# A graph layer's kernel: the edge lists are squeezed in pieces through a PSUM bank, partly in an earlier stage, and ScalarE scales most of the node rows

## The chip, the cores and the metric

One core of one Trainium2 chip runs the whole program. The metric is the device time of one execution, in microseconds; the smaller the better.

## The reference

The layer has 12,500 nodes of 256 features and 212,500 edges, sorted by destination. Every node has a self loop.

```python
deg_out = clip(segment_sum(ones, src), 1)
deg_in  = clip(segment_sum(ones, dst), 1)
h  = feats * rsqrt(deg_out)[:, None]
m  = segment_sum(h[src], dst) * rsqrt(deg_in)[:, None]
x  = (m @ W_gc + b_gc) + (feats @ W_res + b_res)
y  = x + moe_ff(x)              # 64 experts, top 2, capacity 1024, 256 -> 512 -> 256, gelu
y  = (y - mean(y, 0)) * rsqrt(var(y, 0) + eps) * gamma + beta
out = layernorm(feats + y)      # over the features
```

All data are float32 and the indices int32.

## The kernel before

The program goes through five stages, one after the other.

1. Degree stage. The out-degrees are counted with one-hot matrices: VectorE makes `o_hi` and `o_lo` (L204), ScalarE makes `s_lo` (L421), TensorE multiplies them into `deg` and `deg_s`. Meanwhile SP's queue fetches the node features into `acc` (seen as `xs`) and writes zeros to DRAM, for `z_d` and for a strip `lent_d` (L431). At its end a short chain goes from one engine to the next: `s_sb` (L451), a last matmul, `d_out` (L454), a square root on ScalarE and a few small VectorE steps up to `r_out` (L193 to L199). `r_out` holds one over the root of each node's out-degree.
2. h stage. `xs` is multiplied by `r_out` in fifteen pieces of up to seven tiles of 128 nodes. VectorE does ten pieces (L542) and ScalarE five (L540, one instruction for each tile). Each piece is written to `h_d` in DRAM by SP (L544). The edge lists are fetched into a tile `room` (`Lanes.fetch`, L477 to L482), and VectorE runs `fitting` over them, which finds out whether the edges keep to the shape that the fast path needs. Once its rows are written out, `acc` is cleared for the sums (L558), ten parts by GpSimd and four by VectorE. A branch (L562) that is not taken on these data holds the slow path.
3. Edge stage. This is the longest. For each of 1,584 rows of 128 edges, GpSimd issues an indirect DMA (L702) that gathers 128 rows of `h_d` into a ring of six tiles of four rows. VectorE makes a one-hot matrix `o` (L694), 16 rows ahead. TensorE multiplies them into `p` (L716). Twelve rows make a group of nodes; its sums go through `out_of`, `add_own` (L762), `numbers`, `turn` and `to_nodes` (L815) into `acc`. When nodes are complete they go through the dense layer and the router (`nodes`, with L916 reading a PSUM bank), which enters the tokens into a PSUM table `tab` (L1016).
4. The experts, over tokens gathered from DRAM.
5. The two normalisations, and the output.

The edge stage's order is written out by hand in a `manual_schedule`: the loop over rows `c` records `row(c)`, `one_hot(c + 16)` and whatever `at_row` or `later` has put down for that row. The earlier stages are ordered by the scheduler. Every engine runs its own list in order.

The edges fall in two kinds. The first 168 rows (`HC`) are taken as they come. The other 118 groups (`NL`) are "lanes" of 1,620 edges (`L`) on one partition each, from which 84 self loops (`SKIP`) are taken out so that 1,536 edges are left; the self loops are added by `add_own`. That is the squeeze: an edge's source, place and mark are packed into one int32 word, the number of places it has to move is put in the top bits, and for each of seven bits (`BITS`) four operations move the words that have the bit set by 1, 2, 4, ... places. In the kernel before all of it is done in `compact()` (L1024 to L1077), as 46 VectorE steps on whole lanes, with every operand in SBUF. `compact_by` spreads them over the rows 14 to 109 of the edge stage. The lists are fetched a second time for this, into the end of `acc` (`lent`), which is filled from `lent_d` with zeros again at row 138 (L1128). Then TensorE turns the result over (`lay`), and ScalarE writes it to `src_col` and `rel` (`laid`), which the gathers and one-hots of row 168 and later read.

```python
lambda i=i: V.tensor_scalar(m, w, 31 - SHIFT - i, 31,
    op0=ALU.logical_shift_left, op1=ALU.arith_shift_right),
lambda: V.tensor_tensor(b, w, m, op=ALU.bitwise_and),
lambda: V.tensor_tensor(w, w, b, op=ALU.bitwise_xor),
lambda by=by: V.tensor_tensor(w[:, : L - by], w[:, : L - by], b[:, by:], op=ALU.bitwise_or),
```

`tables` is an SBUF tile that the router fills late. Until then parts of it serve as the source of zeros, as room for `own_of` and as room for `shift` in `numbers`.

Of the kernel before, what the change touches and what calls it, by code (L numbers as in the profile page):

```python
# [8 lines left out]
F32 = mybir.dt.float32  # L9
# [10 lines left out]
P = 128  # L20
# [33 lines left out]
ROOM = 3 * L + 2 * HALF  # L54
NC = NG * GR
W = P
# [45 lines left out]
def gnn_moe_kernel(  # L102
# [26 lines left out]
    lent_d = dram.tile([P, ROOM], F32, name="lent_d")  # L129
# [118 lines left out]

    with ExitStack() as stack:
# [24 lines left out]
        for a in range(0, ROOM, 2 * D):  # L274
            n = min(2 * D, ROOM - a)
            zeros.append((lent_d[:, a : a + n], zero[:, :n]))


        def columns():
# [14 lines left out]
            for k, to in enumerate((src_col, rel)):  # L294
                S.copy(to[:, :HC], p[:, k].rearrange("p a c -> p (a c)")[:, :HC])

# [99 lines left out]
        for c0 in range(0, C0 + 1, CH):  # L396
# [16 lines left out]
            for k in range(k0, k1):  # L413
# [23 lines left out]
                if k == 30:  # L437
                    columns()
                if k == 40:
                    windows()  # L440
# [16 lines left out]

    lent = acc[:, 2 * NP - ROOM :]  # L460

    class Lanes:
        def __init__(self, room):
            self.given = [room[:, i * L : (i + 1) * L].bitcast(I32) for i in range(2)]
            self.buf = room[:, 2 * L : 3 * L]

            self.left = room[:, 3 * L : 3 * L + HALF].bitcast(BF16)[:, : L + 1]
            self.at = room[:, 3 * L + HALF :].bitcast(BF16)[:, :L]
            self.is_self, self.again = (
                self.buf.bitcast(BF16)[:, i * L : (i + 1) * L] for i in range(2)  # L470
            )

        def fetch(self):
            b = HE + (NL - 1) * L
            for i, e in enumerate((src, dst)):
                t = self.given[i]
                GP.memset(t, (0, BEHIND)[i])  # L477
                nc.sync.dma_start(t[: NL - 1], e[HE:b].rearrange("(p c) -> p c", c=L))
                nc.sync.dma_start(
                    t[NL - 1 : NL, : M - b], e[b:].rearrange("(p c) -> p c", p=1)  # L480
                )
            GP.memset(self.left, 0.0)  # L482

        def leave_out(self, n_left):

            r = NL
            s, d = (t[:r] for t in self.given)
            is_self, again = self.is_self[:r], self.again[:r]
            return [
                lambda: V.tensor_tensor(is_self, s, d, op=ALU.is_equal),  # L490
                lambda: V.tensor_tensor(again[:, 1:], d[:, 1:], d[:, :-1], op=ALU.is_equal),
                lambda: V.tensor_tensor(again[:, 1:], is_self[:, 1:], again[:, 1:], op=ALU.mult),
                lambda: V.scalar_tensor_tensor(
                    self.left[:r, 1:L], is_self[:, :-1], 0.5, again[:, 1:],
                    op0=ALU.is_lt, op1=ALU.mult, accum_out=n_left[:r],
                ),
                lambda: V.tensor_scalar(
                    self.at[:r], d, n0_lane[:r], 255.0,
                    op0=ALU.subtract, op1=ALU.min,
                ),  # L500
            ]

    def fitting(lanes, n_left):

        r = NL

        def outside(i, lim_of, op):
            V.tensor_scalar(
                lanes.is_self[:r], lanes.at[:r], lim_of, None, op0=op, op1=ALU.add,
                accum_out=bad[:r, 2 + i : 3 + i],  # L510
            )

        def begins():
            junk = lanes.buf[:r, :r]
            V.scalar_tensor_tensor(
                junk, n0_b[:r, 0, HG:], 1.0, ident[:r, :r],
                op0=ALU.mult, op1=ALU.mult, accum_out=n0_lane[:r],
            )

        return [begins] + lanes.leave_out(n_left) + [  # L520
            lambda: outside(0, 0.0, ALU.is_lt),
            lambda: outside(1, float(W), ALU.is_ge),
            lambda: V.tensor_single_scalar(
                bad[:r, 4:5], n_left[:r], SKIP - 0.5, op=ALU.is_lt
            ),
        ]

    with ExitStack() as stack:
        two = stack.enter_context(tc.tile_pool(name="h_two", bufs=2))
        ps2 = stack.enter_context(tc.tile_pool(name="h_ps2", bufs=2, space=PSUM))  # L530
        one = stack.enter_context(tc.tile_pool(name="h_one", bufs=1))
        lanes = Lanes(one.tile([P, ROOM], F32, name="room"))
        lanes.fetch()
        n_left = one.tile([P, 1], F32, name="n_left")
        for i, (t0, n) in enumerate(GROUPS + [(NT - 1, 1)]):
            r = rows(t0)
            xt = xs[:r, t0 : t0 + n]
            if i % 3 == 1:
                for t in range(n):
                    S.activation(xt[:, t], xt[:, t], AF.Copy, scale=r_out[:r, t0 + t : t0 + t + 1])  # L540
            else:
                V.tensor_mul(xt, xt, r_out[:r, t0 : t0 + n, None].to_broadcast([r, n, D]))  # L542
            if r == P:
                nc.sync.dma_start(whole(h_d)[:, t0 : t0 + n], xt)  # L544
            else:
                nc.sync.dma_start(h_d[t0 * P :], xt[:, 0])
        for f in fitting(lanes, n_left):
            f()
# [8 lines left out]
        for i, t in enumerate(range(0, 2 * NT, 14)):  # L557
            (GP if i < 10 else V).memset(acc[:, t * P : (t + 14) * P], 0.0)  # L558
# [3 lines left out]
        with tc.If(unfit > 0):  # L562

# [39 lines left out]
            nc.sync.dma_start(lent_d, lent)  # L603

    lanes = Lanes(lent)
    lanes.fetch()


    with ExitStack() as stack:
# [117 lines left out]
        n_left = one.tile([P, 1], F32, name="n_left")  # L727

# [39 lines left out]
        def numbers(g, s, t):  # L768
            add_own(g, s, t)
            shift = spare[:, (5 + g // 2 % 2) * D : (6 + g // 2 % 2) * D]  # L770
# [74 lines left out]
        def nodes(t0, n, t):  # L845
# [168 lines left out]
            def enter(i, k, at, vals, t):  # L1014
                for m in range(2):
                    T.matmul(  # L1016
                        tab, vals[:r, m], at[:r],
                        start=t0 + i + k + m == 0, stop=t0 + i == NT - 1 and k + m == 2,
                    )
# [4 lines left out]
        def compact():  # L1024

            r = NL
            w, m = (t[:r] for t in lanes.given)
            before_, b, f = m.bitcast(F32), lanes.buf[:r].bitcast(I32), lanes.buf[:r]
            lf, ones_l = lanes.left[:r], lanes.is_self[:r]
            out_steps = lanes.leave_out(n_left) + [  # L1030
                lambda: V.memset(ones_l, 1.0),
                lambda: V.tensor_tensor_scan(
                    before_, ones_l, lf[:, :L], 0.0, op0=ALU.mult, op1=ALU.add
                ),
                lambda: V.scalar_tensor_tensor(
                    lf[:, :L], before_, SKIP + 0.5, lf[:, :L], op0=ALU.is_lt, op1=ALU.mult
                ),

                lambda: V.scalar_tensor_tensor(
                    f, lf[:, 1:], float(MARK), lanes.at[:r], op0=ALU.mult, op1=ALU.add  # L1040
                ),
                lambda: V.scalar_tensor_tensor(
                    w, w, float(2 * MARK), f, op0=ALU.mult, op1=ALU.add
                ),

                lambda: V.tensor_scalar_min(b, before_, float(SKIP)),
                lambda: V.scalar_tensor_tensor(
                    w, b, SHIFT, w, op0=ALU.logical_shift_left, op1=ALU.bitwise_or
                ),
                lambda: V.tensor_scalar_add(b, lf[:, :L], -1.0),  # L1050
                lambda: V.tensor_tensor(w, w, b, op=ALU.bitwise_and),
            ]
            for i in range(BITS):
                by = 1 << i
                out_steps += [
                    lambda i=i: V.tensor_scalar(
                        m, w, 31 - SHIFT - i, 31,
                        op0=ALU.logical_shift_left, op1=ALU.arith_shift_right,
                    ),
                    lambda: V.tensor_tensor(b, w, m, op=ALU.bitwise_and),  # L1060
                    lambda: V.tensor_tensor(w, w, b, op=ALU.bitwise_xor),
                    lambda by=by: V.tensor_tensor(
                        w[:, : L - by], w[:, : L - by], b[:, by:], op=ALU.bitwise_or
                    ),
                ]
            full = slice(0, GR * P)
            out_steps += [
                lambda: V.tensor_scalar(
                    m[:, full], w[:, full], 9, (1 << 14) - 1,
                    op0=ALU.arith_shift_right, op1=ALU.bitwise_and,  # L1070
                ),
                lambda: V.tensor_single_scalar(
                    b[:, full], w[:, full], 2 * MARK - 1, op=ALU.bitwise_and
                ),
                lambda: V.tensor_copy(before_[:, full], m[:, full]),
                lambda: V.tensor_copy(f[:, full], b[:, full]),
# [458 lines left out]
```

## Time and profile before

| | us |
|---|---|
| median of 3 runs | 3423.75 (3421.28 to 3424.61) |
| the profiled execution | 3423.65 |
| its span, first to last instruction | 3421.9 |
| first gather of the edge stage issued (L702) | 246.66 |
| last gather issued | 2282.63 |
| VectorE busy over the span | 1641.3 (48%) |
| GpSimd busy over the span | 2051.2 (60%) |
| TensorE busy over the span | 2685.0 (78%) |

The profile gives, for each engine, the busy time in forty slices of the span; for each group of instructions (a source line, an engine, an operation and a shape) the count, the busy time and the mean; and what ended the idle time before them. The trace behind it can be listed instruction by instruction. PE is TensorE, DVE is VectorE, ACT is ScalarE, POOL is GpSimd, and SP is the queue that issues most transfers. PEclk is the granted TensorE clock as a share of full speed. An indirect DMA shows as a POOL instruction for the time that GpSimd takes to issue it, not for the transfer.

### The profile page before, as it was taken

Reading aid. Unit: us, or ns where it says so; the run is one execution under the profiler, and the core shown is the slowest. Engines: PE = TensorE matmul, PEld = TensorE weight load, DVE = VectorE, ACT = ScalarE, POOL = GpSimd, SP = SyncE. Lnnn points to the kernel's source line nnn. Section 1 sums busy time; section 2 is a strip of 40 time slices with the busy share of each in tenths; the row PEclk is TensorE's granted clock in tenths of the full one; section 3 lists DMA queues with packets and bytes.
Section 4 is the critical chain, followed back from the end, with each engine's and each line's share of the span. In section 5 each row is a group of like instructions: output and inputs, shape, how many; then the busy total and the mean of one; then the engine's idle time right before and its main releaser. Section 6 shows DMA issues by size and latency. Waiting matters only on the chain. (4 is left out here: it accounts for less than half of the span.)

```text
span 3421.9 us, 36966 instructions
## 1 busy us (share of the span) xinstructions
PE 2685.0 (78%) x11059; PEld 1778.3 (52%) x11121; DVE 1641.3 (48%) x6013; ACT 707.9 (21%) x1994; POOL 2051.2 (60%) x2092
## 2 busy tenths in 40 slices
PE   6826777777787777777777778876999999999644
PEld 5612344444454544444444445554778766778533
DVE  9975534455445445545454455664222212222498
ACT  8930010000010000000000000111222211222368
POOL 0038877777777777777777777754555555554100
PEclk8755578888888888888888988888999999999865
DMA  9462244444444444444444444433344444566677
GB/s 356 158 200 77 85 156 123 125 126 127 128 126 126 127 124 126 128 129 126 122 129 126 126 127 130 131 97 119 111 131 126 133 153 154 178 183 203 214 221 238
DMA packets 257102, 498.19 MB, mean 146 GB/s; under 512 B 44567, under 2 KB 169109, under 8 KB 248578
## 3 DMA queue, kind: packets, MB, share of 16 engines
q0 software_dynamic: 98800, 264.95, 26.8%
q1 hardware_dynamic: 144800, 218.02, 19.5%
q10 hardware_dynamic: 13298, 12.80, 1.2%
q8 instruction: 91, 1.49, 0.2%
q14 instruction: 113, 0.93, 0.1%
HBM read 402.59 MB, written 96.44 MB: 146 GB/s over the span
## 5 line engine op out<-in xcount | busy, mean ns | idle before, releaser
L702 POOL DMA_INDIRECT ring<-h_d,src_col x1584 | 1553.8, 981 | 483.3 <-issue 424.6
L716 PE MATMUL p<-ring,o 128*128 128x258 f32 x3168 | 1207.3, 492 | 473.2 <-DMA ring<-h_d,src_col 436.8
L716 PEld LDWEIGHTS p<-ring,o 128*128 128x128 f32 x3168 | 619.0, 227 | 976.8 <-DMA ring<-h_d,src_col 666.0
L694 DVE TENSOR_SCALAR o<-lane,rel 128x128 f32<-128x128 f32 x1584 | 380.8, 303 | 617.4 <-PE p L716 617.3
L1275 PE MATMUL yp<-w,h 128*128 128x256 f32 (+3 forms) x1928 | 432.9, 380 | 0.0
L1231 POOL DMA_INDIRECT xg<-x_d,tables x241 | 233.0, 967 | 333.1 <-PE xtp L1246 219.4
L1259 PE MATMUL hp<-xT,w 128*128 128x384 f32 (+11 forms) x1328 | 399.4, 454 | 1.4 <-DVE xT L1250 1.4
L1275 PEld LDWEIGHTS yp<-w,h 128*128 128x128 f32 (+3 forms) x1928 | 341.3, 181 | 65.0 <-issue 7.3
L751 ACT COPY s<-p 128x258 f32<-128x258 f32 x132 | 49.4, 374 | 1325.1 <-PE p L716 1325.1
L1263 ACT ACTIVATE h<-hp,w 128x384 f32<-128x384 f32 (+11 forms) x332 | 181.2, 546 | 669.6 <-PE hp L1259 668.8
L1259 PEld LDWEIGHTS hp<-xT,w 128*128 128x128 f32 x1328 | 248.0, 191 | 131.6 <-issue 57.0
L1281 POOL DMA_INDIRECT z_d<-yo,tables x241 | 238.1, 988 | 121.9 <-DVE yo L1280 66.1
L1250 DVE COPY xT<-xtp 128x768 f32<-128x768 f32 (+2 forms) x83 | 77.4, 932 | 405.2 <-PE xtp L1246 405.2
L1280 DVE TENSOR_TENSOR yo<-yp,bb 128x256 f32<-128x256 f32 (+3 forms) x241 | 102.0, 423 | 276.3 <-PE yp L1275 268.5
L421 ACT ACTIVATE s_lo<-lane_b,nb 128x128 bf16<-128x128 bf16 x581 | 171.1, 389 | 4.4 <-DVE lo_end L412 1.8
L1016 PE MATMUL tab<-at,vals 128*128 128x512 bf16 x330 | 130.2, 471 | 18.2 <-DVE vals L1009 7.7
L815 DVE TENSOR_TENSOR acc<-q,acc 128x256 f32 x132 | 55.8, 423 | 165.5 <-PE q L792 122.0
L902 PE MATMUL bank<-wcat,acc 128*128 128x320 f32 x392 | 132.6, 464 | 0.0
L907 PE MATMUL bank<-wcat,xT 128*128 128x320 f32 x392 | 124.4, 440 | 0.0
L477 POOL MEMSET room<- 128x1620 int32 x2 | 2.8, 1447 | 192.7 <-DVE r_out L199 192.7
L711 ACT CAST ring<-mark 128x4 f32<-128x4 bf16 x354 | 57.8, 197 | 260.1 <-issue 260.0
L423 PE MATMUL deg<-o_hi,o_lo 128*128 128x98 bf16 x1079 | 79.9, 237 | 24.6 <-DVE o_lo L204 22.1
(280 smaller groups left out, 2583.8 us busy)
## 6 DMA issues: line engine op xcount, KB each, us to landing
w<-in_wpack SPq DMA_DIRECT2D x64, 1026.0 KB
ring<-h_d,src_col POOLq DMA_INDIRECT x1584, 2.8
z_d<-tables SPq DMA_DIRECT2D x98, 256.0 KB
zt<-z_d SPq DMA_DIRECT2D x24, 1024.0 KB
tables<-h_d SPq DMA_DIRECT2D x118, 128.0 KB
xt<-in_x ACTq DMA_DIRECT2D x48, 256.0 KB
x_d<-y SPq DMA_DIRECT2D x48, 256.0 KB
z<-in_x SPq DMA_DIRECT2D x12, 1024.0 KB
```

Of the source, the lines that this page charges most:

```text
L421: S.activation(s_lo[:, i], lane_b, AF.Sign, bias=nb[:, k, i : i + 1])
L694: o_last[u] = V.tensor_scalar(o_of[u][:, j], lane, rel[:, c : c + 1], None, op0=ALU.is_equal)
L702: i = GP.indirect_dma_start(out=r[:, k, :D], out_offset=None, in_=h_d, in_offset=bass.IndirectOffsetOnAxis(ap=src_col[:, c : c + 1], axis=0),)
L716: i = T.matmul(p_of[g], o_of[v][:, n], r[:, k], start=j == 0, stop=j == GR - 1)
L902: T.matmul(gps[i][:r], acc2[:, k, a : a + r], wcat[:, k], start=k == 0, stop=False,)
L907: T.matmul(gps[i][:r], v["xT"][:, i, k, :r], wcat[:, 2 + k], start=False, stop=k == 1,)
L1016: T.matmul(tab, vals[:r, m], at[:r], start=t0 + i + k + m == 0, stop=t0 + i == NT - 1 and k + m == 2,)
L1231: GP.indirect_dma_start(out=g, out_offset=None, in_=x2_d, in_offset=bass.IndirectOffsetOnAxis(ap=at[:, 0, k : k + 1], axis=0),)
L1259: T.matmul(hp[:, :m], w1[:, c, j * P : (j + 1) * P], xT[:, c, :m], start=c == 0, stop=c == 1,)
L1263: S.activation(h1[:, j, :m], hp[:, :m], AF.Gelu, bias=w[:, 2 * H + 4 * D + j : 2 * H + 4 * D + j + 1],)
L1275: T.matmul(yp[:r], h1[:, j, k * P : k * P + r], w2[:, j], start=j == 0, stop=j == 3,)
L1281: st = GP.indirect_dma_start(out=z_d, out_offset=bass.IndirectOffsetOnAxis(ap=at[:r, 1, k : k + 1], axis=0), in_=yo[:r], in_offset=None, b ...
```

## The change

- The edge lists are fetched once, in the degree stage (`lines`, after step 65 of 83), `src` into `tables` and `dst` into a tile of its own. The two fetches into `room` and `lent`, with their GpSimd memsets, go.
- `leave_out` and `fitting` stay in the h stage. The rest of the preparation (`marked`) and the first bit of the squeeze move there too.
- Bits 2 to 7 stay in the edge stage, spread from row 0 to row 109, but a lane is worked in four pieces of 512, 512, 512 and 84 columns, and the intermediate `q` is the PSUM bank `tab`, which the router uses only later. That makes 96 VectorE steps in place of 24. The results are taken out in six pieces: VectorE writes to the bank and ScalarE copies it to SBUF.
- In the h stage VectorE scales two pieces (three and seven tiles) and ScalarE the other 88 tiles. GpSimd clears the first 70 tiles' worth of `acc`; the last 7,168 columns (`late`) are not cleared but filled with zeros from DRAM at row 138, where 6,482 were filled before.
- `numbers` uses one buffer for `shift` in place of two while the lanes lie in `tables`.

The order of VectorE's list at the end of the degree stage differs as well, since the scheduler sets it. In the kernel before, it is `s_sb`, `d_out`, the steps to `r_out`, the ten multiplications, and then `leave_out` and `fitting`. In the changed kernel the steps alternate:

```
L204 o_lo (the last)          L498 again*is_self   118x1619
L487 n0_lane                  L196 rsq_q
L494, L495 memsets of left    L499 left            118x1619
L491 at_w        118x1620     L197 rsq_q
L468 s_sb                     L507 outside (1)     118x1620
L496 is_self     118x1620     L198 rsq_q
L471 d_out                    L507 outside (2)     118x1620
L497 again       118x1619     L199 r_out
L194 reciprocal               L511 bad, L519 memset of is_self, L564 two multiplications
```

The core of the diff:

```diff
-ROOM = 3 * L + 2 * HALF
+LATE = 28 * 256
...
+        def lines():
+            b = HE + (NL - 1) * L
+            for t, e, v in ((l_src, src, 0), (l_dst, dst, BEHIND)):
+                GP.memset(t[:, M - b :], v)
+                nc.sync.dma_start(t[: NL - 1], e[HE:b].rearrange("(p c) -> p c", c=L))
+                nc.sync.dma_start(
+                    t[NL - 1 : NL, : M - b], e[b:].rearrange("(p c) -> p c", p=1)
+                )
...
+                if k == 65:
+                    assert not zeros
+                    lines()
...
+    def squeeze(bit, a, n, q):
+        by = 1 << bit
+        lo = max(a, by)
+        w = l_w[:, a : a + n]
+        return [
+            lambda: V.tensor_scalar(
+                q, w, 31 - SHIFT - bit, 31, op0=ALU.logical_shift_left, op1=ALU.arith_shift_right
+            ),
+            lambda: V.tensor_tensor(q, w, q, op=ALU.bitwise_and),
+            lambda: V.tensor_tensor(w, w, q, op=ALU.bitwise_xor),
+            lambda: V.tensor_tensor(
+                l_w[:, lo - by : a + n - by], l_w[:, lo - by : a + n - by], q[:, lo - a :],
+                op=ALU.bitwise_or,
+            ),
+        ]
...
-        lanes = Lanes(one.tile([P, ROOM], F32, name="room"))
-        lanes.fetch()
...
-        for i, (t0, n) in enumerate(GROUPS + [(NT - 1, 1)]):
+        pieces = [(0, 3), (3, 4)] + GROUPS[1:] + [(NT - 1, 1)]
+        for i, (t0, n) in enumerate(pieces):
...
-            if i % 3 == 1:
+            if i in (0, 2):
+                V.tensor_mul(xt, xt, r_out[:r, t0 : t0 + n, None].to_broadcast([r, n, D]))
+            else:
                 for t in range(n):
                     S.activation(xt[:, t], xt[:, t], AF.Copy, scale=r_out[:r, t0 + t : t0 + t + 1])
...
-        for f in fitting(lanes, n_left):
-            f()
+        leave_out()
+        fitting()
...
-        for i, t in enumerate(range(0, 2 * NT, 14)):
-            (GP if i < 10 else V).memset(acc[:, t * P : (t + 14) * P], 0.0)
+        for a in range(0, 2 * NP - LATE, 14 * P):
+            GP.memset(acc[:, a : a + 14 * P], 0.0)
+        marked()
+        for f in squeeze(0, 0, L, before_.bitcast(I32)):
+            f()
...
-    lanes = Lanes(lent)
-    lanes.fetch()
+    line_stack.close()
...
+        scratch = tab.bitcast(I32)
+        l_out = [late[:NL, k * GR * P : (k + 1) * GR * P] for k in range(2)]
+        def squeeze_all():
+            steps_of = []
+            for i in range(1, BITS):
+                for a in range(0, L, 4 * P):
+                    n = min(4 * P, L - a)
+                    steps_of += squeeze(i, a, n, scratch[:NL, :n])
+            for a in range(0, GR * P, 4 * P):
+                v = slice(a, a + 4 * P)
+                for k, to in enumerate(l_out):
+                    q = scratch[:NL]
+                    steps_of += [
...
+                        lambda v=v, q=q, to=to: S.copy(to[:, v], q),
+                    ]
...
-            steps_of = compact()
+            steps_of = squeeze_all()
...
-                at_row(14 + (c - 14) * i / len(steps_of), lambda t, f=f: f())
+                at_row(c * i / len(steps_of), lambda t, f=f: f())
...
-            at_row(c + 3 * len(lays) + LAG, lambda t: nc.sync.dma_start(lent, lent_d))
+            at_row(c + 3 * len(lays) + LAG, lambda t: nc.sync.dma_start(late, late_d))
```

## The prediction

> **What bounds the kernel now.** I read the forty slices first: GpSimd is busy seven tenths from slice 3 to slice 26, which is the edge stage. Then the groups, for what GpSimd does there.
>
> ```profile
> POOL 0038877777777777777777777754555555554100
> L702 POOL DMA_INDIRECT ring<-h_d,src_col x1584 | 1553.8, 981 | 483.3 <-issue 424.6
> ```
>
> A gather takes 0.95 us and 0.30 us pass before the next ("issue": GpSimd waits for nothing that is shown), so a row costs 1.25 us. TensorE's two matmuls for a row do not set this: most of TensorE's idle time before L716 is put down to the gathers. To see where the stage falls short of that pace I counted gathers in stretches (columns: stretch, length, POOL busy and count, PEclk, DMA share, GB/s).
>
> ```profile
> 246.60:426.70 180.10, 146.59 (x110) 0.58 0.30 87
> 600.00:760.00 160.00, 121.31 (x128) 0.84 0.44 125
> ```
>
> 128 gathers take 160 us in the steady part, 1.25 us each. The first 110 take 180.1 us in place of 137.5: 42.6 us are lost. The timeline of GpSimd and VectorE shows how.
>
> ```profile
> 258.64 1.85 DVE L490 TENSOR_TENSOR acc<-acc 118x1620 bf16<-118x1620 int32 x1
> 259.41 1.89 POOL L702 DMA_INDIRECT ring<-h_d,src_col  x1 [0.31 <-issue]
> 260.99 1.84 DVE L491 TENSOR_TENSOR acc<-acc 118x1619 bf16<-118x1619 int32 x1
> 261.61 2.03 POOL L702 DMA_INDIRECT ring<-h_d,src_col  x1 [0.30 <-issue]
> ...
> 299.34 1.00 DVE L1050 TENSOR_SCALAR acc<-acc 118x1620 int32<-118x1620 bf16 x1
> 299.54 1.61 POOL L702 DMA_INDIRECT ring<-h_d,src_col  x1 [0.30 <-issue]
> ```
>
> A gather whose start falls inside a squeeze step ends about 0.81 us after that step (260.49 to 261.30, 262.83 to 263.64, 300.34 to 301.15). The steps hold GpSimd up. This stage is bound by GpSimd plus what VectorE takes from it, so the squeeze is on the path though VectorE has time to spare. Does a PSUM operand change that? Two neighbouring gathers, outside the squeeze:
>
> ```profile
> 597.94 0.42 DVE L815 TENSOR_TENSOR acc<-q,acc 128x256 f32 x1
> 598.00 0.94 POOL L702 DMA_INDIRECT ring<-h_d,src_col  x1 [0.30 <-issue]
> ...
> 599.25 1.44 POOL L702 DMA_INDIRECT ring<-h_d,src_col  x1 [0.30 <-issue]
> 599.30 0.49 DVE L762 SCALAR_TENSOR_TENSOR s<-tables,s 128x256 f32<-128x256 f32 x1
> ```
>
> L815 reads PSUM (`q`) and SBUF, writes SBUF, and covers the start of a gather: 0.94 us. L762 reads two SBUF tiles: 1.44. Over the trace I find 29 gathers whose start lies under an L815 (mean 0.947 us), 11 under an L916, which also reads a bank (0.947), and 18 under an L762 (1.14). The last view is the h stage, which the first gather waits for.
>
> ```profile
> 190.50 0.26 DVE L451 COPY s_sb<-deg_s 128x98 f32<-128x98 f32 x1 [1.36 <-PE deg_s L425]
> 194.25 0.26 DVE L199 TENSOR_TENSOR r_out<-rsq_r,rsq_q 128x98 f32<-128x98 f32 x1
> 194.54 13.67 ACT L540 ACTIVATE acc<-acc,r_out 128x256 f32<-128x256 f32 x34 [1.97 <-DVE r_out L199]
> 240.25 1.55 DVE L558 MEMSET acc<- 128x1792 f32 x1 [0.98 <-DMA h_d<-acc]
> 241.97 2.98 POOL L477 MEMSET acc<- 128x1620 int32 x2 [11.24 <-DVEq L562]
> 244.89 1.59 POOL L482 MEMSET acc<- 128x1621 bf16 x1
> 246.66 1.16 POOL L702 DMA_INDIRECT ring<-h_d,src_col  x1 [0.17 <-POOL acc L482]
> ```
>
> `r_out` is ready at 194.51. The writing of `h_d` keeps the DMA engines full until about 240, and then three GpSimd memsets, which prepare the second fetch of the lists, stand ahead of the first gather.
>
> **The change, part by part.** Times are on the clock of the profiled execution, 3423.65 us by its own time, 1.75 over its span and 0.1 under the median of 3423.75.
>
> *Squeeze in the rows.* It removes from the rows all 46 whole-lane steps. It adds 96 steps in the bank and six that write the bank for ScalarE to copy. Each of the 102 has one operand in SBUF and the rest in PSUM. The XOR and OR steps (read both, write SBUF) are L815's kind, and by its row cost the gathers nothing. The AND reads both and writes PSUM: fewer SBUF accesses, the same. The 30 TENSOR_SCALAR steps that go from SBUF to PSUM have no row. Bounds: 0, as L815; and, if they hold GpSimd as L1050 did, about half the starts covered (0.61 of 1.25 us) by some 0.4 us for 24 long ones, 5 us. The nearest row by length is L1107, a TENSOR_SCALAR of 512 within SBUF (0.43 us at 449.39): the two gathers whose start it covers take 0.95. I take 0. [...] I add 0.5 us for short overlaps. The gain is 42.6 - 0.5 = 42.1 us.
>
> *Is VectorE fast enough?* After L815's 256 columns the next instruction starts 0.33 us later (597.94 to 598.27); whole-lane steps of 1,620 do so after 1.75 us (L491 to L490 at 212.50 and 214.25), 1.08 ns a column, so 256 columns more make 0.61. So 78 steps of 512 take 48 us and 24 of 84 some 4. One-hots: 109 at 0.25 (0.20 apart in a burst, 0.30 by their row's mean), 27. The groups' own work (L773 to L820): 8. Six waits for ScalarE's copies, about 1 us each. In all some 93 us in 136 us of rows. [...] One-hots are made 16 rows ahead, 20 us, so a wait of a microsecond for a copy reaches nobody. ScalarE's six copies (about 0.6 us, as L891's 0.59 for 512 columns) stand before `s` copies that are 11 rows late by design.
>
> *h stage, the start.* Now the order of VectorE's list counts. Between the last `o_lo` (ends 189.14) and `r_out` there stand eight steps that were behind the multiplications before. With their durations from `fitting` in this trace: `n0_lane` 0.2, memsets 0.1 and `at_w` 1.0 end at 190.4, ahead of `s_sb`'s wait, free. `is_self` 1.76 ends at 192.5 and `d_out` follows (191.86 before) to 192.75; `again` to 194.5, over the square root; reciprocal to 195.3; `again*is_self` 1.1 and L196 to 196.7; `left` 1.9 and L197 to 198.9; two `outside` of 1.85 with L198 and L199 to 203.1. `r_out` is 8.6 us later: a cost that the diff does not show. All wait for it: ScalarE's first tile and SP's first write of h.
>
> *h stage, the rest.* ScalarE scales 88 tiles at 13.67/34 = 0.402 us: 35.4 us, to 238.5. VectorE has a memset (1.4), two multiplications (2.5), then `marked` (a scan of 3.5, five steps of 1.84, two of 1.0) and four steps of the squeeze (6.5): it ends near 229, off the path. The DMA engines had 14.3 MB here in about 41 us; the 1.5 MB of lists have moved to step 65, about 155 us, when the DMA share is 0.07 and the zeros have long left SP's queue (last issue 124). The 12.8 MB of h now need 36 to 37 us from about 206: to 242.5. So both ScalarE and the transfers end at about the same time; after ScalarE's last tile there is an issue (0.3), 0.8 MB (2.1) and the landing, for which I use a gather's 2.8 less its 0.4 of data, 2.4: 243.3. The first fetch of `xt` now stands in ScalarE's list behind the tiles (it was at 190.54) and takes 0.25 MB's share, 0.4. The three memsets (4.6) are gone, and so are VectorE's four. First gather: 243.8, against 246.66. Gain 2.9.
>
> *The refill.* SP brings 3.67 MB for 3.32 at row 138. At that point one gather stood 0.9 us behind a DMA; 0.1 more. One `shift` buffer in place of two, used every 24 rows: 0.
>
> Sum: 42.1 + 2.9 - 0.1 = 44.9 us, 3423.65 - 44.9 = 3378.75; I say 3379. After row 110 GpSimd keeps its 1.25 us to the last gather, so the shift reaches the end whole.
>
> **The rivals.** *The 30 new SBUF-to-PSUM steps, or all short steps, still hold GpSimd in part* (chance 0.10). L762's 0.19 us a covered start speaks for it, L815 against. At 0.19 us for half of 102 starts it is 10 us: 3389.
>
> *The h stage comes out later than worked out* (0.12). ScalarE and the transfers are coupled with no slack: if each piece waits for both, the first gather comes at 249, and the change gives 40: 3384. Against it: VectorE's two pieces put 21 tiles ahead at the start. It could also be earlier by 3 us, 3376, which I count with the main case.
>
> *Slower: the bank does not free GpSimd, because the other operand is still in SBUF, and steps and gathers fall into step with each other* (0.04). There is about one step for each row. If each start met one and paid L762's worst 0.5 us, 102 of them would cost 51 us in place of 42.6, and with the h stage at 249 the time would be 3434. It decides from 0.44 us a row (44.9 over 102); chance overlaps alone, half the starts and 0.3 left of each, give 0.15 and stay faster. L815's 29 cases speak against.
>
> *It does nothing* (0.01): then VectorE would have to be the bound, 1.25 us of work in each row more than it has.
>
> **How the numbers follow.** Main case 0.73, 3379, itself good for 6 us either way: 3 from the h stage, 3 from one execution against another (the runs before spread by 3.3). The range goes down to 3371 and up to 3390, which takes in both of the faster rivals. A measurement can tell about 0.2%, 7 us: faster 0.95, same 0.01, slower 0.04.
>
> **What would show it.** L702's mean near 950 ns from the first row (981 before), and row 110 issued 137.7 us after the first. `r_out` near 203, ScalarE's tiles ending near 238.5, the first gather at 243 to 245. L548 and L549 near 0.7 us each. I am wrong if gathers under the bank's steps take over 1.1 us, if GpSimd waits for TensorE in the first 110 rows, or if the first gather comes after 248.

## The result, and the profile after

| | before | changed | |
|---|---|---|---|
| median of four runs, us | 3424.18 (3421.28 to 3425.38) | 3382.00 (3381.02 to 3382.28) | ratio 0.9879, 95% interval 0.9867 to 0.9890 |
| profiled execution, us (span) | 3423.65 (3421.9) | 3381.99 (3380.1) | 41.7 shorter |

The changed kernel is 42 us faster; 3379 was predicted. First the same views as before: the slices, the gathers' group (now L729), and the stretches of 110 and 128 gathers. The stretches are given for L729 alone: stretch, length, POOL busy and count, PEclk, DMA share, GB/s.

```profile
POOL 0027777777777777777777777735555555554100
L729 POOL DMA_INDIRECT ring<-h_d,src_col x1584 | 1511.0, 954 | 495.3 <-issue 425.3
```

```profile
244.46:382.60 138.14, 104.62 (x111) 0.65 0.36 106
600.00:760.00 160.00, 121.31 (x128) 0.91 0.44 128
```

The mean gather fell from 981 to 954 ns, and the first 110 rows from 180.1 to 138.1 us. At 1.25 us a row they would take 137.5, so 0.6 us is left of the 42.6 that were lost. GpSimd still sets the pace: of its 495.3 us of idle time before the gathers 425.3 are put down to "issue", and the steady part still takes 1.25 us a row. The gathers have become shorter, the idle 0.30 us between them is the same. The timeline of GpSimd and VectorE shows steps that write the bank (L544, L547) and steps that read it (L548) over the starts of gathers:

```profile
248.39 0.69 DVE L544 TENSOR_SCALAR tab<-tables 118x512 int32<-118x512 int32 x1
248.48 0.95 POOL L729 DMA_INDIRECT ring<-h_d,src_col  x1 [0.30 <-issue]
249.18 0.69 DVE L547 TENSOR_TENSOR tab<-tables,tab 118x512 int32<-118x512 int32 x1
249.73 0.95 POOL L729 DMA_INDIRECT ring<-h_d,src_col  x1 [0.30 <-issue]
...
246.81 0.68 DVE L548 TENSOR_TENSOR tables<-tables,tab 118x512 int32<-118x512 int32 x1
247.23 0.94 POOL L729 DMA_INDIRECT ring<-h_d,src_col  x1 [0.30 <-issue]
```

50 of the first 110 gathers start under one of the steps of the squeeze (each counted under the step that began last); they take 0.945 to 0.946 us in the mean of each kind, as the 42 that start under no VectorE work do. The 0.6 us that is left has a source too. 16 gathers start under a one-hot (L721), a step within SBUF; those take 0.98 us in the mean, which makes 0.6 us together:

```profile
245.82 0.28 DVE L721 TENSOR_SCALAR o<-lane,rel 128x128 f32<-128x128 f32 x1
245.90 1.03 POOL L729 DMA_INDIRECT ring<-h_d,src_col  x1 [0.30 <-issue]
```

The h stage and the refill, from the timelines of all engines and of GpSimd:

```profile
188.07 0.26 DVE L204 TENSOR_TENSOR o_lo<-lane_b,lo_end 128x128 bf16<-128x128 bf16 x1
200.82 0.26 DVE L199 TENSOR_TENSOR r_out<-rsq_r,rsq_q 128x98 f32<-128x98 f32 x1
...
413.94 0.95 POOL L729 DMA_INDIRECT ring<-h_d,src_col  x1 [0.30 <-issue]
417.50 0.94 POOL L729 DMA_INDIRECT ring<-h_d,src_col  x1 [2.62 <-DMA ring<-h_d,src_col]
```

The last `o_lo` and row 136 in the kernel before:

```profile
188.91 0.23 DVE L204 TENSOR_TENSOR o_lo<-lane_b,lo_end 128x128 bf16<-128x128 bf16 x1
...
460.69 0.94 POOL L702 DMA_INDIRECT ring<-h_d,src_col  x1 [1.23 <-DMA ring<-h_d,src_col]
```

`r_out` is ready 12.8 us after the last `o_lo`, where it took 5.4. At row 136 a gather stands 2.3 us longer than the usual 0.30 behind a transfer; before it was 0.9.

From `r_out` to the first gather 43.4 us pass, where it was 52.2. This is where the kernel before ends its transfers of `h_d` (columns: stretch, length, then PE, PEld, DVE, ACT, POOL busy and count, PEclk, DMA share, GB/s):

```profile
238.00:239.00 1.00, 0.00 (x0) 0.00 (x0) 1.00 (x1) 0.00 (x0) 0.00 (x0) 0.50 0.78 245
239.00:240.00 1.00, 0.00 (x0) 0.00 (x0) 0.27 (x1) 0.00 (x0) 0.00 (x0) 0.50 0.06 22
```

They end near 239.1, and the first gather comes 7.6 us later, after VectorE's last part of the clearing and GpSimd's three memsets. In the changed kernel they end near 242.4 (shown below), and the gather comes 2.1 us later. So some 5.5 of the 8.8 us lie behind the transfers, and 3.2 in the transfers, from which the 1.5 MB of the lists are gone.

Where the 41.8 us of span come from, read by the clocks of the two traces at the same row:

| | gain so far, us |
|---|---|
| first gather (246.66, now 244.46) | 2.20 |
| row 110 (426.75, now 382.59) | 44.16 |
| row 134, ahead of the refill's gap | 44.58 |
| row 136 | 43.19 |
| last gather (2282.63, now 2239.09) | 43.54 |
| first gather of the experts (2336.12, now 2295.43) | 40.69 |
| end of the span | 41.8 |

### The profile page after: what moved, and what is told of

Its sections match the earlier page's. It is cut to its first block, busy times and chain, and to the rows that moved or that the text cites. A ratio compares the mean times of both kernels' runs of the same rounds, so it can differ in the third digit from the quotient of the medians.

```text
span 3380.1 us, 37103 instructions
## 1 busy us (share of the span) xinstructions
PE 2658.2 (79%) x11121; PEld 1756.8 (52%) x11121; DVE 1620.7 (48%) x6071; ACT 732.6 (22%) x2054; POOL 2001.5 (59%) x2088
## 3 DMA queue, kind: packets, MB, share of 16 engines
q1 hardware_dynamic: 144696, 217.20, 19.5%
## 5 line engine op out<-in xcount | busy, mean ns | idle before, releaser
L729 POOL DMA_INDIRECT ring<-h_d,src_col x1584 | 1511.0, 954 | 495.3 <-issue 425.3
L743 PE MATMUL p<-ring,o 128*128 128x258 f32 x3168 | 1179.6, 482 | 481.8 <-DMA ring<-h_d,src_col 400.1
L743 PEld LDWEIGHTS p<-ring,o 128*128 128x128 f32 x3168 | 603.5, 222 | 976.5 <-DMA ring<-h_d,src_col 647.2
L721 DVE TENSOR_SCALAR o<-lane,rel 128x128 f32<-128x128 f32 x1584 | 384.3, 302 | 591.5 <-PE p L743 591.3
L1043 PE MATMUL tab<-at,vals 128*128 128x512 bf16 x392 | 139.7, 447 | 11.6 <-DVE vals L1031 11.6
L583 POOL MEMSET acc<- 128x1792 f32 x10 | 17.5, 1754 | 213.7 <-DMA h_d<-acc 213.7
L928 PEld LDWEIGHTS bank<-wcat,acc 128*128 128x128 f32 x392 | 83.5, 213 | 32.4 <-issue 7.3
```

Of the source, the lines that this page charges most:

```text
L721: o_last[u] = V.tensor_scalar(o_of[u][:, j], lane, rel[:, c : c + 1], None, op0=ALU.is_equal)
L729: i = GP.indirect_dma_start(out=r[:, k, :D], out_offset=None, in_=h_d, in_offset=bass.IndirectOffsetOnAxis(ap=src_col[:, c : c + 1], axis=0),)
L743: i = T.matmul(p_of[g], o_of[v][:, n], r[:, k], start=j == 0, stop=j == GR - 1)
L928: T.matmul(gps[i][:r], acc2[:, k, a : a + r], wcat[:, k], start=k == 0, stop=False,)
L1043: T.matmul(tab, vals[:r, m], at[:r], start=t0 + i + k + m == 0, stop=t0 + i == NT - 1 and k + m == 2,)
```

## The experiments

Theory: VectorE steps whose operands are all in SBUF hold a gather up, and the bank (with the move of half the work) ends that. The rivals: the cutting into pieces did it, or the move; and, for the h stage, that ScalarE's share ended it. Three versions take the gain in the rows apart, four the h stage, one the refill; one joins two of them, and the kernel before was traced once more. The versions were run in three groups, each beside the kernel before on the same chip, which had medians of 3421.70 (scratch, half, `r_out`, split), 3425.38 (whole lanes, refill, both, before again) and 3708.57 us (four pieces, two queues).

**The scratch back in SBUF.**

```diff
-        scratch = tab.bitcast(I32)
+        scratch = late[:, 3072:3584].bitcast(I32)
```

> One line of the changed kernel is altered: the scratch of the squeeze in the rows is 512 columns of SBUF (an unused part of late) in place of the PSUM bank. The pieces, their number and their rows stay. Theory (the bank frees GpSimd): the 72 AND, XOR and OR steps now have two SBUF inputs like L762, which cost 0.19 us for each gather start that it covered with 0.49 us; for pieces of about 0.6 us, half the starts covered and some 0.25 us each, the first 110 gathers lose some 10 us (5 to 20; up to 39 if steps and gathers fall into step), row 110 comes about 148 us after the first gather (138.1 in the changed kernel), and the time is near 3392. Rival (what helped was the cutting into 512 columns, or the move of the other half to the h stage, and the bank is idle decoration): row 110 at 138 to 139 us, 3382 to 3383.

Measured: 3387.10 us median, ratio 0.9898 (0.9882 to 0.9915). The first 110 rows take 145.1 us, 7.0 more than with the bank. Its timeline shows what the bank had kept away:

```profile
246.91 0.68 DVE L547 TENSOR_TENSOR acc<-tables,acc 118x512 int32<-118x512 int32 x1
247.03 1.39 POOL L729 DMA_INDIRECT ring<-h_d,src_col  x1 [0.30 <-issue]
...
258.66 1.24 POOL L729 DMA_INDIRECT ring<-h_d,src_col  x1 [0.30 <-issue]
258.66 0.42 DVE L544 TENSOR_SCALAR acc<-tables 118x512 int32<-118x512 int32 x1
...
254.35 0.68 DVE L549 TENSOR_TENSOR tables<-tables,acc 118x512 int32<-118x512 int32 x1
254.56 1.29 POOL L729 DMA_INDIRECT ring<-h_d,src_col  x1 [0.30 <-issue]
```

All three gathers end 0.82 or 0.83 us after the step that covered their start (247.59 to 248.42, 259.08 to 259.90, 255.03 to 255.85). In the changed kernel no gather that starts under a step of the squeeze alone is held. So the bank's effect is real; but it is 7 us of 42, the lower part of what was expected, and the larger part must lie elsewhere.

**The moved half back in the rows.**

```diff
-        marked()
-        for f in squeeze(0, 0, L, before_.bitcast(I32)):
-            f()
...
+    l_dst = late[:, 2 * GR * P : 2 * GR * P + L].bitcast(I32)   # dst fetched again; l_buf, left, at_w in late too
...
-            steps_of = []
+            steps_of = leave_out() + marked() + squeeze(0, 0, L, before_.bitcast(I32))
```

> The part of the squeeze that the change put into the h stage (marked and the first bit, with the five steps of leave_out that they need repeated) goes back to the rows, as whole-lane steps of 1,620 columns in SBUF; dst is fetched again into late for it. Bits 2 to 7 stay in the bank in pieces. Theory (every whole-lane SBUF step costs the gathers 42.6/46 = 0.93 us): 18 such steps, 16.7 us, row 110 at 155 us after the first gather, and the time near 3399, so that the bank's pieces account for the other 25 us of the gain. Rival (the bank did nearly all, the steps in the h stage were cheap ones): under 5 us, 3387 at most. Rival (the move did nearly all): over 35 us, 3417 or more.

Measured: 3391.97 us median, ratio 0.9912 (0.9896 to 0.9929). The rows take 153.3 us, 15.2 more: 0.84 us for each of the 18 steps. (The profiled execution of this version, 3400.2 us, is its slowest; the rows after 136 took 3.7 us more in it, so its median is the figure for the time.) Both rivals fall; the move is worth a third.

**Whole lanes in SBUF, the move kept.**

```diff
-        scratch = tab.bitcast(I32)
+        scratch = late[:, 2 * GR * P : 2 * GR * P + L].bitcast(I32)
...
-                for a in range(0, L, 4 * P):
-                    n = min(4 * P, L - a)
-                    steps_of += squeeze(i, a, n, scratch[:NL, :n])
+                steps_of += squeeze(i, 0, L, scratch[:NL])
...
```

> The changed kernel with bits 2 to 7 of the squeeze in whole-lane steps of 1,620 columns and their scratch in SBUF (both the bank and the cutting undone); the part that moved to the h stage stays there. Theory (cutting is the larger part: with the scratch in SBUF but in pieces the first 110 rows took 145.1 us, with the other half back in the rows 153.3, against 138.1 with all of the change and 180.1 before it; 180.1 - 15.2 = 164.9): row 110 comes 162 to 167 us after the first gather, of which about 20 us are the cutting and 7 the bank; time near 3408. Rival (the three parts are not additive, and the steps in the rows before were dear only because all 46 followed one another): row 110 at 145 to 152 us, under 3396.

Measured: 3407.57 us median, ratio 0.9951 (0.9934 to 0.9968); 163.5 us for the rows. The stretch of 110 gathers in the three versions, in this order: scratch in SBUF, half back in the rows, whole lanes (columns: stretch, length, then PE, PEld, DVE, ACT, POOL busy and count, PEclk, DMA share, GB/s).

```profile
245.41:390.54 145.13, 120.96 (x242) 55.40 (x242) 75.47 (x252) 6.87 (x16) 111.63 (x111) 0.58 0.34 101
```

```profile
243.49:396.83 153.34, 117.90 (x241) 54.81 (x242) 111.88 (x273) 6.52 (x15) 119.81 (x111) 0.60 0.33 97
```

```profile
244.75:408.26 163.51, 131.25 (x242) 58.51 (x242) 69.96 (x176) 6.22 (x12) 129.99 (x111) 0.52 0.30 89
```

POOL's busy time carries all of it: 111.6, 119.8 and 130.0 us against 104.6. VectorE's does not: in the last version it is the least busy of the three (70.0 us) and the rows are the longest. Cutting alone, at the same place and in SBUF, is worth 163.5 - 145.1 = 18.4 us; then the bank 7.0; and the move 15.2. Together 40.6 of the 42.0 measured; the remainder is what the parts do to each other.

Why cutting helps so much can be worked out from the 0.82. A gather takes 0.95 us anyway, so a step of length d adds the time by which it outlasts the gather's start, less 0.13. A step shorter than the pace of 1.25 us meets a start with chance d/1.25, and costs (d - 0.13)²/2.5 on average: 0.12 us for a piece of 0.68. The 54 AND, XOR and OR pieces of 512 columns make 6.5 us, the 18 TENSOR_SCALAR of 0.42 another 0.6; measured 7.0. A whole-lane step of 1.84 always meets a start, and outlasts it by 0.59 to 1.84 us, 1.08 after the 0.13 is taken off: 18 of them 19.5 us, and eight shorter ones of about 0.3 make 22, measured 25.4. This is an estimate that takes the phases as random, which they are not quite.

It also leaves out a second way to hold a gather, which the whole lanes show. Here the start lies under no step; a TENSOR_SCALAR of a whole lane begins while the gather is under way, and the gather ends 0.12 us after it:

```profile
285.63 1.62 POOL L729 DMA_INDIRECT ring<-h_d,src_col  x1 [0.30 <-issue]
286.13 1.00 DVE L544 TENSOR_SCALAR acc<-tables 118x1620 int32<-118x1620 int32 x1
```

In the kernel before, 11 of the first 110 gathers end in this way, behind a TENSOR_SCALAR or a CAST of about 1 us; beyond the first way it makes some 6 of the 42.6 us (an estimate: each end against 0.82 us after the step that covered the start, or against 0.95 us in all). In the changed kernel there is none.

**`r_out` first.**

```diff
     def leave_out():
 
+        V.tensor_copy(l_buf[:, :1], r_out[:NL, :1])
+        V.tensor_copy(l_buf[:, L - 1 :], r_out[:NL, :1])
```

> Two copies of one column of r_out into l_buf stand ahead of leave_out, so that its steps and fitting must wait for r_out and VectorE's list has s_sb, d_out and the steps to r_out without the eight whole-lane steps between them. Theory (from r_out on, the h stage is bound by the transfers of h_d at 338 GB/s: 12.8 MB in 37.9 us, after 3.4 us for the first piece): r_out near 193.7 in place of 201.1, ScalarE's last tile near 229, the first gather near 237.1 in place of 244.5, and the time 7.4 us shorter, near 3374.6. Rival (something else ends the stage, GpSimd's clearing of the sums or the branch behind VectorE's 28 us of leave_out, marked and squeeze): the first gather at 240 to 244, gain under 4 us.

Measured: 3370.79 us median, ratio 0.9850 (0.9834 to 0.9867). Timeline of all engines:

```profile
192.06 0.26 DVE L199 TENSOR_TENSOR r_out<-rsq_r,rsq_q 128x98 f32<-128x98 f32 x1
192.36 12.07 ACT L569 ACTIVATE acc<-acc,r_out 128x256 f32<-128x256 f32 x30 [1.97 <-DVE r_out L199]
195.56 1.84 DVE L499 TENSOR_TENSOR l_buf<-l_dst 118x1619 bf16<-118x1619 int32 x1
...
234.79 1.18 POOL L731 DMA_INDIRECT ring<-h_d,src_col  x1 [10.98 <-DVE o L723]
```

`r_out` comes 8.8 us earlier and the first gather 9.7; both more than expected. The eight steps now run behind `r_out`, where VectorE had time to spare. It ends at 230.7, and the transfers of `h_d` at 232.9. So the changed kernel gives away some 10 us of its own gain by the place of these steps in VectorE's list.

**The split of the scaling as before.**

```diff
-        pieces = [(0, 3), (3, 4)] + GROUPS[1:] + [(NT - 1, 1)]
+        pieces = GROUPS + [(NT - 1, 1)]
...
-            if i in (0, 2):
+            if i % 3 != 1:
```

> In the h stage VectorE multiplies ten pieces and ScalarE 35 tiles in five pieces, as in the kernel before; all else is the changed kernel. Theory (the stage is bound by the transfers once r_out is there): ScalarE's tiles end by 240, VectorE's marked and first bit end near 243 (nine pieces of 2.02 and one of 0.42, then 21.8 us), first gather 244 to 245.5 where the changed kernel has 244.5; time within 1 us of 3382. Rival (ScalarE's 35 us of tiles ended the stage in the changed kernel): the first gather comes at 241 or earlier, 3379 or less. Rival (VectorE needs to be unburdened): the first gather later than 247.

Measured: 3380.62 us median, ratio 0.9880 (0.9863 to 0.9896), level with the changed kernel. (ScalarE's five pieces are 34 tiles: four of seven and one of six.) The first gather is at 246.24, 44.4 us after `r_out` where the changed kernel needs 43.4. That is 0.7 later than the theory's bound; `r_out` itself came 0.7 later in this execution. ScalarE's last tile ends at 215.5, 20.8 us earlier, and the gather does not come earlier for it; the rival that ScalarE ended the stage falls. These are the last microseconds of the transfers, in the changed kernel, here, and with `r_out` first (columns as above):

```profile
241.00:242.00 1.00, 0.00 (x0) 0.00 (x0) 0.65 (x14) 0.00 (x0) 0.00 (x0) 0.50 1.07 363
242.00:243.00 1.00, 0.00 (x0) 0.00 (x0) 1.00 (x6) 0.00 (x0) 0.00 (x0) 0.50 0.39 125
243.00:244.00 1.00, 0.00 (x0) 0.00 (x0) 1.00 (x6) 0.00 (x0) 0.00 (x0) 0.50 0.00 0
```

```profile
243.00:244.00 1.00, 0.00 (x0) 0.00 (x0) 0.23 (x9) 0.00 (x0) 0.00 (x0) 0.50 0.87 250
244.00:245.00 1.00, 0.00 (x0) 0.00 (x0) 1.00 (x11) 0.00 (x0) 0.00 (x0) 0.50 0.08 28
```

```profile
232.00:233.00 1.00, 0.00 (x0) 0.00 (x0) 1.00 (x10) 0.00 (x0) 0.00 (x0) 0.50 0.82 258
233.00:234.00 1.00, 0.00 (x0) 0.00 (x0) 1.00 (x6) 0.00 (x0) 0.00 (x0) 0.50 0.02 6
```

The share of the DMA engines falls to nothing near 242.4, 244.0 and 232.9, read off these shares; the first gather follows 2.1, 2.2 and 1.9 us later. It follows no other engine's end so evenly: VectorE's work on the lanes ended 17.2, 3.3 and 4.1 us before it.

```profile
246.24 1.16 POOL L729 DMA_INDIRECT ring<-h_d,src_col  x1 [10.36 <-DVE o L721]
```

The view puts the gather's wait down to `o`, but no gather reads `o`; a wait for several semaphores is put down to one of them.

**Four pieces on VectorE, and the same with two queues.** Both on a chip where the kernel before takes 3708.57 us.

```diff
-            if i in (0, 2):
+            if i in (0, 2, 4, 6):
...
-                nc.sync.dma_start(whole(h_d)[:, t0 : t0 + n], xt)
+                q = nc.sync if i in (0, 2, 4, 6) or i % 4 == 1 else nc.scalar    # two queues only
+                q.dma_start(whole(h_d)[:, t0 : t0 + n], xt)
```

> The changed kernel with four pieces (24 tiles) of the scaling on VectorE and 74 on ScalarE, in place of two and 88; the control for the next run. Theory (the transfers of h_d end the stage, at 338 to 346 GB/s from SP's queue): ScalarE's tiles end near 231, VectorE near 231, the first gather 43 to 44.5 us after r_out as in the changed kernel (43.4) and with the split of before (44.4). Rival (ScalarE's 2.8 us for each piece paces the issues, and that pacing, not the engines, makes the 338 GB/s): the first gather 3 us or more earlier.

> As the control, but six of the pieces that ScalarE scales are written to h_d by ScalarE's own queue, the other ten by SP's. In three traces the writes go at 338 to 350 GB/s and for some microseconds at 375 to 389, the faster stretch each time some 5 us after a transfer from ScalarE's queue (xt) or, in the kernel before, after the lists. Theory (one queue's writes go at 340, two queues' at 380): 12.8 MB in 33.5 us, first gather 39 to 40 us after r_out, 4 us earlier than the control, and the time 3 to 4 us shorter. Rival (the rate does not depend on the queue): first gather within 1 us of the control's.

Measured: 3681.76 us (ratio 0.9926, 0.9909 to 0.9942) and 3684.31 us (0.9933, 0.9916 to 0.9949), level. The first gathers come 43.1 and 43.6 us after `r_out`. Three divisions of the scaling now give 43.1, 43.4 and 44.4, so ScalarE's pace matters by 1 us at most; and the second queue brings nothing, so that theory falls. The rate, in the same stretch of the control and of the two queues:

```profile
235.00:240.00 5.00, 0.00 (x0) 0.00 (x0) 0.00 (x0) 0.00 (x0) 0.00 (x0) 0.50 1.06 364
```

```profile
235.00:240.00 5.00, 0.00 (x0) 0.00 (x0) 0.00 (x0) 0.00 (x0) 0.00 (x0) 0.50 1.04 343
```

This chip shows something else. Its mean granted clock is 0.79, where the changed kernel's trace had 0.866, and the ratio is 0.993 in place of 0.988. The gathers themselves are as short as in the changed kernel, yet the rows are longer (stretch of the first 110, control):

```profile
244.29:399.68 155.39, 101.21 (x233) 53.93 (x233) 74.30 (x219) 3.59 (x9) 104.70 (x111) 0.62 0.32 94
L729 POOL DMA_INDIRECT ring<-h_d,src_col x1584 | 1513.1, 955 | 781.9 <-issue 444.0
```

1.41 us a row with POOL busy for 104.7: GpSimd waits here, 781.9 us over the kernel against 495.3; 94.6 of it is put down to `p` (41.4 in the changed kernel's trace), and 177.3 to something that the profile cannot name. GpSimd no longer sets the pace alone, so shorter gathers can be worth less. That this is all of the smaller ratio is not shown: there is no trace of the kernel before at this clock.

**The refill in fourteen.**

```diff
-            at_row(c + 3 * len(lays) + LAG, lambda t: nc.sync.dma_start(late, late_d))
+            for i, a in enumerate(range(0, LATE, 4 * P)):
+                v = slice(a, a + 4 * P)
+                at_row(c + 3 * len(lays) + LAG + 12 * i,
+                       lambda t, v=v: nc.sync.dma_start(late[:, v], late_d[:, v]))
```

> The zeros for late are brought by 14 transfers of 512 columns, one every 12 rows from row 138 on, in place of one of 7,168 columns. Theory (the 3.67 MB stand ahead of a gather's rows in the DMA engines' queues, which made the gather of row 136 come 2.3 us late): the gap at row 135 to 136 is gone and the other 13 transfers of 0.26 MB show no gap over 0.3 us each, so that rows 134 to 160 take 2.3 us less; time near 3380. Rival (the gap is another wait at this row, or each transfer makes a gap of its own): the gap stays over 1.5 us or fourteen gaps add up to 2 us or more; 3382 or later.

Measured: 3381.04 us median, ratio 0.9874 (0.9858 to 0.9891). The times cannot tell 2 us; the trace can. Rows 134 to 136 take 2.70 us (4.81 in the changed kernel), and no gap over 0.5 us is left in the rows up to 411:

```profile
412.69 0.94 POOL L729 DMA_INDIRECT ring<-h_d,src_col  x1 [0.30 <-issue]
413.94 0.95 POOL L729 DMA_INDIRECT ring<-h_d,src_col  x1 [0.30 <-issue]
417.50 0.94 POOL L729 DMA_INDIRECT ring<-h_d,src_col  x1 [2.62 <-DMA ring<-h_d,src_col]
```

```profile
411.92 0.95 POOL L729 DMA_INDIRECT ring<-h_d,src_col  x1 [0.30 <-issue]
413.17 1.15 POOL L729 DMA_INDIRECT ring<-h_d,src_col  x1 [0.30 <-issue]
414.62 0.95 POOL L729 DMA_INDIRECT ring<-h_d,src_col  x1 [0.30 <-issue]
```

The first fence is the changed kernel, the second this one, at the same rows. So the gap came from the one large transfer.

**Both.** The diffs of `r_out` first and of the refill in one kernel.

> Both together: r_out ahead of leave_out and fitting, and the refill in 14 transfers. The two lie in different stages, so the gains should add: 10.5 us (as 3381.2 in the mean of the two undisturbed versions against 3370.8) and 2.3 us, which makes some 3369 on the chip on which the kernel before takes 3421.7. If the refill's gap is only where the wait for some other thing shows, 3371.

Measured: 3371.75 us median, ratio 0.9847 (0.9830 to 0.9863) against 3425.38; the changed kernel's ratio is 0.9879. It is the best of the versions by its ratio, with `r_out` first alone at 0.9850, from which it can't be told; its interval lies below the changed kernel's, and that of `r_out` first touches it. The traces show both parts: first gather at 235.46, rows 134 to 136 in 2.50 us.

**The kernel before again.**

> The kernel before, unchanged, for a second trace. In its first trace 53.5 us pass from the last gather of the edge stage to the first gather of the experts; in five traces of the changed kernel and its variants it is 55.4 to 57.0. Theory (the change costs 2 to 3 us here by some way not known): 53.5 again, within 0.7. Rival (one execution differs from another here): 55 or more.

Measured: one time, 3428.74 us, and a trace. It repeats the first 110 rows at 181.0 us. From the last gather to the experts' first it shows 55.4 us; its first trace showed 53.5. So 1.9 of the 2.85 us that the changed kernel seemed to lose there is within what two executions of one kernel differ by. Eight traces of the changed kernel and its versions, without the two of the last group, lie between 55.3 and 57.3, 56.3 in the mean, against 54.4 for the two of the kernel before. A loss of 1 to 2 us remains possible; it is left open.

## Why the prediction was right, point by point

*The rows: right in size, and only in part for the reason given.* 42.1 us were forecast, 42.0 came. That bank steps cost the gathers nothing was right, the 30 TENSOR_SCALAR steps included, and GpSimd's idle time stayed at 0.30 us a row, so that it did not wait for TensorE there. But the prediction gave the bank as the reason why the 102 new steps cost nothing, and never asked what the pieces would do with their scratch in SBUF. Cutting alone brings 18 of the 25 us that the cutting and the bank gain together. The total was safe from this, since whichever part did it, nothing was left to lose. Its counts of covered gathers do not all come out again: over the whole trace, each gather put to the step that began last, they are 29 under an L815, 29 under an L916 (not 11) and 24 under an L762 (not 18), with means of 0.945, 0.945 and 1.11 us. The reading stands.

*A row misread.* The prediction took L1107, 0.43 us within SBUF, as evidence that short TENSOR_SCALAR steps do not hold a gather. The two gathers it read start at 449.31 and 465.69; the steps start at 449.39 and 465.73. They cover no start at all, and they end 0.4 us or more before the gathers would have ended anyway, too early to hold them in the second way. Where a TENSOR_SCALAR of 512 columns within SBUF does cover a start (0.42 us, L544 at 258.66, above), the gather ends 0.82 us after it. For the price it made no difference: the TENSOR_SCALAR steps that write the bank held no gather (0.945 to 0.946 us).

*VectorE's cover: held.* 512 columns in the bank take 0.67 to 0.71 us by their rows, where 0.61 was estimated, the copies' steps 0.74; VectorE is busy 82.5 us of the 138.1, under the forecast 93. The bank lengthens one kind of step: the TENSOR_SCALAR of 512 takes 0.42 us within SBUF and 0.70 into the bank, TENSOR_TENSOR 0.68 within SBUF and 0.68 to 0.71 with the bank.

*`r_out` 8.6 us later: the mechanism right, the size about so.* It was ready at 201.08, 6.6 us later than in the trace before; counted from the last `o_lo`, which ended 0.8 us earlier in this execution, 7.4 later; and 8.8 later than in the version with `r_out` first. The diff does not show this cost; VectorE's list does.

*First gather 243.8, measured 244.46.* The step that failed is the one that let ScalarE and the transfers end together. Only the transfers end this stage: 338 GB/s for most of it, and some 2 us from their end to the gather. The forecast's 36 to 37 us for h were 38 to 39. The near hit is in part luck: `r_out` came 2.0 us earlier than forecast, and from there to the gather it took 43.4 us in place of 40.7. The other case named there, each piece waiting for both and 249, did not come. Nor did ScalarE's 88 tiles bring anything that the time shows: with 34 it is the same.

*The refill: the mis-sized term.* 0.1 us more was forecast from 10% more bytes; it cost 1.4 more in this trace (2.31 against 0.92). In the traces with the single transfer this gap is 1.2 to 2.3 us after the change and 0.9 and 1.2 before, so about a microsecond seems to be the change's and the rest chance; why 10% more bytes should cost that is not shown.

*The tail was not in the sum.* "The shift reaches the end whole" held to the last gather (43.5). Of the 2.85 us after it 1 to 2 may be the change's, as above, and the rest is the spread of executions.

So the sum was 44.9 and the trace says 41.8: 0.7 lost at the first gather, 1.3 at the refill and 2.85 ahead of the experts, and 1.8 gained elsewhere, 1.1 of it behind the first gather of the experts.

## What to carry to other kernels

When one engine's steps hold up another's through SBUF, ask for the length of the step before its place: by the estimate above, what one step below the other's pace costs grows about with the square of its length, so the same work in short pieces costs less in sum (7.0 us in place of 25.4 here), and a PSUM bank removed those 7.0. Read the order of an engine's list around the value that the next stage waits for; work that fits "beside" it can stand in front of it, and two one-column copies moved 10 us here. And a split between engines is worth little where the transfer behind it sets the end (the first gather 43.1, 43.4 and 44.4 us after `r_out` in three splits).

## What the runs showed of the hardware

VectorE steps within SBUF hold a gather in two ways. One whose start such a step covers ends 0.82 us after the step, whether that is a TENSOR_TENSOR of 1.84 us, one of 0.68, a TENSOR_SCALAR of 0.42 or a one-hot of 0.28; the scan of 3.5 us gave 0.75. One that is under way when a TENSOR_SCALAR or CAST of 1 us begins ends 0.12 us after that step. Of the first 110 gathers in the kernel before, 38 took over 0.96 us: 25 the first way (three of them behind a step that began up to 0.1 us after the start), 11 the second, one under the scan and one, 0.98 us long, in a burst of one-hots. Of the gathers in the changed kernel that began under a step with an operand in the bank, and under no one-hot, none took over 0.95 us.

The writes of `h_d` go at 340 GB/s or so for most of the time and at 375 to 390 for some microseconds, with the DMA engines' share over 1 in both (about 1.03 and 1.09 in the changed kernel). The fast stretches lie from 237 to the end in the changed kernel, from 216 to 221 with the split as before, from 227 to 232 with `r_out` first, from 231 to 236 with four pieces, from 205 to 221 in the kernel before. In the first four the fast stretch begins 4 to 6 us after ScalarE issued the one transfer of `xt`; with two queues, whose `xt` came last, there is none. What sets the rate stays open; at 383 all through, the h stage would be some 4 us shorter (an estimate: 12.8 MB at 338 and at 383).
